# Planned order for SyncE and GpSimd, and the local maxima's transfers moved to GpSimd's queue, in a fused attention and feed-forward kernel

## The chip, the core and the metric

The kernel runs on one core of a Trainium2 chip, with one launch. The metric is the device time in microseconds; lower is better. Engines are named as in the profile: PE (TensorE matmuls), PEld (TensorE weight loads), DVE (VectorE), ACT (ScalarE), POOL (GpSimd), SP (SyncE, which issues nearly all transfers). A "q" behind an engine's name stands for the engine's queue, in which it waits and from which it issues.

## What is computed

A layer norm of `x` (4096 rows of 256) feeds two branches, and both are added to `x`.

The first branch is attention with 16 heads of 16 columns over all 4096 keys, with a softmax over a rational function of the scores:

```python
attn = jnp.einsum('bqhd,bkhd->bhqk', q, k)
sq = attn * attn
w = sq / (nsum - 2.0 * sq + EPS)
w = jax.nn.softmax(w, axis=-1)
out = jnp.einsum('bhqk,bkhd->bqhd', w, v).reshape(B, S, D)
```

The second branch is a two-layer network on the same rows: windowed attention (8 heads of 64, windows of 128 rows that look one window back), then a gated feed-forward with 682 hidden columns, each with a residual.

## The kernel before, in words

**Prologue** (lines 358 to 574, the first 240 us): layer norm, `q`, `k` and `v` of the first branch, stored to DRAM in the layouts that the main part reads.

**Main part.** The first branch is cut into 512 tiles (16 heads, 32 blocks of 128 queries), each in two halves of 2048 keys. For one half: PE makes scores in PSUM (`scores`, L951), ACT squares them into `r` (L955), DVE subtracts 1 (L959), and DVE and ACT together form the weight's exponent in `u` (L963, L972, L978, L981, L985). DVE's `weights` (L993) multiplies and keeps a running maximum in a column of `mm`. When both halves are done, the row maximum of the tile is known, one number for each of 128 queries.

PE turns the exponents round (`turn`, L1014 and L1017): a bf16 matmul first fills the PSUM bank with minus the maximum, and four transposes add the values. For that the maximum is needed as a row, in three bf16 pieces. `maximum` (L998 to L1007) makes it: a transfer of the upper half of the number into row 0 of `mrow`, a subtraction on POOL that leaves the rest, a second transfer, a second subtraction, a third transfer. So a tile has a chain DVE L993, SP, POOL L1007, SP, POOL L1007, SP, PE L1014. ACT then takes the exponential (L1025) and PE multiplies with `v` (`values`, L1036). After four tiles ACT copies the sum to `ob` (L1043) and SP stores it (L1045).

**The second branch** runs through the same engines at the same time, as one long chain of steps (`ffn`, L596 to L915, then `finals`). In its windowed attention, `looked` makes the scores of two heads for 256 rows and DVE (L740) adds a mask and keeps the minimum of the negated scores in `mx`, four columns. POOL splits those minima into three bf16 pieces with four operations (L745 to L748, tiles `fm` and `fmd`), SP moves each piece into a row of `frow` (L751, three transfers), and PE uses `frow` in `summed` (L760) as it uses `mrow` in `turn`. There are 128 such groups: 2 layers, 16 blocks of 256 rows, 4 pairs of heads. The step that uses `frow` is not planned earlier than 10 us after the group (`held[c] = P, mT, plan.now + 10000.0`).

**What sets the order.** A planner written in Python (`Plan`) holds a list of tasks with assumed durations, ranks and buffers, and lets them run on assumed engines when the program is built. It emits each task's instructions at the moment it starts. Tasks for PE, ACT and DVE stand in the program in that order, since the three engines are under `manual_schedule` (L1165). Tasks of the kind "X" take no engine in the plan: `maximum` is one, with 6 us from the weights' end until `turn` may start (`MAX_NS`). SP and POOL are not under the manual schedule before the change. A scheduler of the framework, with a cost model of its own, places their instructions, so their order in the queue is not the order in which the plan emits them.

An engine serves its queue in order. If the first instruction waits, all behind it wait too.

Of the kernel before, what the change touches and what calls it, by code (L numbers as in the profile page):

```python
# [23 lines left out]
NG = S // 512  # L24
# [158 lines left out]
def plan_all(plan, acts, chain, halves):  # L183

    R, PS, U, PE2, PF = Pool(R_BUFS), Pool(3), Pool(U_BUFS), Pool(PE_BUFS), Pool(1)
    acts.pools = dict(r=R, pt=PS, u=U, pe=PE2)
    nothing = lambda: None
    load = [0.0, 0.0]
    subs, last = {}, {"S": None, "P": None, "W": None, "copy": None}

    def rest(i, subs):
        paired = load[0] > load[1]
        load[0] += 10844 if paired else 14448
        load[1] += 12321 if paired else 9050
        acts.mode(i, paired)
        add, D, L, T = plan.add, 2 * i + RANK["D"], 2 * i + RANK["L"], 2 * i + RANK["T"]
        ready = []
        if paired:
            t = add("DVE", 2203, lambda: acts.product(i), D, subs, takes=[(U, i)])
            t = add("DVE", 1135, lambda: acts.positive(i, 0), D, [], [t])  # L200
            t = add("ACT", 1802, lambda: acts.log(i, 0), L, [t])
            t = add("ACT", 1802, lambda: acts.power(i, 0), L, [t])
            ready = [add("DVE", 2203, lambda: acts.signed(i), D, [t])] * 2
        else:
            for h in range(2):
                t = add("DVE", 1135, lambda h=h: acts.positive(i, h), D + h, [subs[h]], [t] if h else [], takes=[] if h else [(U, i)])
                p = add("ACT", 1802, lambda h=h: acts.log(i, h), L + h, [t])
                ready.append(add("ACT", 1802, lambda h=h: acts.power(i, h), L + h, [p]))
        w = None
        for h in range(2):  # L210
            w = add("DVE", 2255, lambda h=h: acts.weights(i, h), T + h, [ready[h]], [w], gives=[(U, i)] if h else [])
        m = add("X", MAX_NS, lambda: acts.maximum(i), 2 * i, [w])
        for n in (2 * i, 2 * i + 1):
            soft(n, m)

    def soft(n, m):
        i, half = divmod(n, 2)
        exps = []
        for z in range(2):
            w = plan.add("PE", 427 + 8 * 109, lambda z=z: acts.turn(n, z), n + RANK["W"] + 0.3 * z, [m], [last["W"]],  # L220
                         takes=[(PS, (n, z, 1))], gives=[(R, n)] if z else [])
            last["W"] = w
            e = plan.add("ACT", 905, lambda z=z: acts.exp(n, z), n + RANK["E"] + 0.3 * z, [w], takes=[(PE2, (n, z))], gives=[(PS, (n, z, 1))])
            exps.append(e)
        fresh = [last["copy"]] if half == 0 and i % 4 == 0 else []
        last["P"] = plan.add("PE", 874, lambda: acts.values(n), n + RANK["P"], exps + fresh, [last["P"]],
                             gives=[(PE2, (n, 0)), (PE2, (n, 1))], mode="C")
        if half and i % 4 == 3:
            last["copy"] = plan.add("ACT", 465, lambda: acts.copied(i), n + RANK["O"], [last["P"]])

    def begin(n):
        sq = []
        for z in range(2):
            s = plan.add("PE", 427, lambda z=z: acts.scores(n, z), n + RANK["S"], [], [last["S"]],
                         takes=[(PS, (n, z, 0))] if z else [(R, n), (PS, (n, z, 0))])
            last["S"] = s
            sq.append(plan.add("ACT", 905, lambda z=z: acts.square(n, z), n + RANK["Q"], [s], gives=[(PS, (n, z, 0))]))
        subs[n] = sub = plan.add("DVE", 1135, nothing, n + RANK["D"], sq, [subs[n - 1]] if n % 2 else [])

        def emit():  # L240
            acts.less(n)
            if n % 2:
                rest(n // 2, [subs.pop(n - 1), subs.pop(n)])
            if n + 8 < halves:
                begin(n + 8)
        sub.emit = emit

    for n in range(min(8, halves)):
        begin(n)

    spent = [0.0]

    def follow(t, step):
        if step is None:
            return
        eng, ns, mode, take, give, at = step
        if eng in ("ACT", "DVE"):
            load[0 if eng == "ACT" else 1] += ns
        due = halves * spent[0] / CHAIN_NS
        spent[0] += ns * PACE[eng]  # L260
        bank = {0: [], 1: [(PF, 0)], 2: [(PS, "f")]}
        u = plan.add(eng, ns, nothing, due + RANK["F"], [t], takes=bank[int(take)], gives=bank[int(give)], mode=mode, at=at)

        def emit():
            follow(u, next(chain, None))
        u.emit = emit

    follow(None, next(chain))
    plan.run()
# [3 lines left out]
def tile_yat_attention_and_local_ffn(ctx: ExitStack, tc: tile.TileContext, io, out):  # L273
# [322 lines left out]
    def ffn():  # L596
        for l in range(DEPTH):
# [63 lines left out]
            for g in range(NGF):  # L661
# [42 lines left out]
                for b in range(2):  # L704
# [4 lines left out]
                                 start=k == 0, stop=k == 1)  # L709
                    yield step("DVE", 600, give=True)  # L710
                    V.tensor_copy(va[:, (2 * g + b) % 3, :, 0:FD], pv.rearrange("p (h d) -> p h d", h=FH))
                if g + 1 < NGF:
                    nxt = fetch(g + 1)
                osum = fa.tile([128, 2, INNER], F32, name="xm2")

                def looked(c):

                    P = fb.tile([128, 2, 2, 256], F32, name="P")
                    mx = fb.tile([128, 4], F32, name="mx")

                    yield step("PE", 1200, "R", take=2)
                    pss = ps_s.tile([128, 2, 2, 256], F32, name=acts.name("pt", "f"))
# [14 lines left out]
                    for e in range(2):  # L737
                        for b in range(2):
                            mk = msk[:, 0 if (g == 0 and b == 0) else 1]
                            V.tensor_tensor_reduce(P[:, e, b], pss[:, e, b], mk, rn[:, 0, b, 2 * c + e:2 * c + e + 1], 3.0e38,  # L740
                                                   ALU.add, ALU.min, mx[:, 2 * e + b:2 * e + b + 1])
                    yield step("X", 0)
                    m3 = fb.tile([128, 3, 4], BF, name="fm3")
                    md = fb.tile([128, 4], F32, name="fmd")
                    G.tensor_copy(m3[:, 0], mx)  # L745
                    G.tensor_tensor(m3[:, 1], mx, m3[:, 0], ALU.subtract)
                    G.tensor_tensor(md, mx, m3[:, 0], ALU.subtract)
                    G.tensor_tensor(m3[:, 2], md, m3[:, 1], ALU.subtract)  # L748
                    mT = frow[c % 2]
                    for c_ in range(3):  # L750
                        nc.sync.dma_start(mT[c_:c_ + 1], m3[:, c_])  # L751
                    held[c] = P, mT, plan.now + 10000.0

                def summed(c):
# [28 lines left out]
                for c in range(5):  # L783
                    if c < 4:
                        yield from looked(c)
                    if c:
                        yield from summed(c - 1)
                oT = fa.tile([128, 4, GT], F32, name="qT")
# [13 lines left out]
                yield step("DVE", 600, give=True)  # L802
                xm = fa.tile([128, 2, D], F32, name="xm")
                V.tensor_tensor(xm, pw, xres, ALU.add)
                nc.sync.dma_start(xm_d[l][g * GT + 1:(g + 1) * GT + 1].rearrange("(t p) c -> p t c", p=128), xm)

            if l == DEPTH - 1:
# [21 lines left out]
            for g in range(NG):  # L829
# [13 lines left out]
                hn = fa.tile([128, 4, D], F32, name="qT")  # L843
                for t in range(4):
                    V.tensor_scalar(hn[:, t], xh[:, t], mv[:, t, 0:1], rstd[:, t:t + 1], ALU.subtract, ALU.mult)
                if g + 1 < NG:
                    nxt = shifted(g + 1)
                h2 = []
                for c in range(2):
                    yield step("PE", 510, take=True)  # L850
# [3 lines left out]
                    yield step("DVE", 725, give=True)  # L854
                    h2.append(fb.tile([128, 512], F32, name="pT"))
                    V.tensor_scalar(h2[c], ph, lngb[:, 0, c:c + 1], lngb[:, 1, c:c + 1], ALU.mult, ALU.add)
                gg = fa.tile([128, 6, 512], F32, name="kv")

                def up(s_, m):
# [36 lines left out]
                if l < DEPTH - 1:  # L896
                    for c in range(2):
# [4 lines left out]
                        yield step("DVE", 600, give=True)  # L902
                        xoT = fb.tile([128, 512], F32, name="pT")
                        V.tensor_copy(xoT, ph)
                        for z in range(2):
                            nc.sync.dma_start(xT_d[l + 1][2 * g + z][c * 128:(c + 1) * 128], xoT[:, z * GT:(z + 1) * GT])
                    for z in range(2):
                        nc.sync.dma_start(xres_d[l + 1][2 * g + z].rearrange("(t p) c -> p t c", p=128), xo[:, 2 * z:2 * z + 2])
                else:
# [2 lines left out]
                    nc.sync.dma_start(xin, acc_d[g].rearrange("(t p) c -> p t c", p=128))  # L912
                    yield step("DVE", 1135)
                    V.tensor_tensor(xo, xo, xin, ALU.add)
                    nc.sync.dma_start(ff_d[g].rearrange("(t p) c -> p t c", p=128), xo)  # L915


# [5 lines left out]
    class Acts:  # L923
# [11 lines left out]
        def scores(self, n, z):  # L935
            i, half = divmod(n, 2)
            h, qt = tiles[i]
            if half == 0 and z == 0:
                if qt == 8 and h + 1 < H:
                    assert self.valued >= 8 * NT * h  # L940
                    load_k(h + 1)
                    load_v(h + 1)
                if qt % 4 == 0 and i // 4 + 1 < len(quads):
                    load_q(*quads[i // 4 + 1])
            if z == 0:
                self.r[n] = hr.tile([128, 2048], F32, name=self.name("r", n))
# [93 lines left out]
        def copied(self, i):  # L1040
            h, qt = tiles[i]
            self.ob = hp.tile([128, 512], F32, name="ob", bufs=1)
            A.copy(self.ob, pav)  # L1043
            if i + 1 < len(tiles):
                nc.sync.dma_start(o_d[qt // 4][h], self.ob)  # L1045
                if h == H - 1:
# [115 lines left out]

    plan = Plan()
    acts = Acts()
    with tc.manual_schedule(engines={mybir.EngineType.PE, mybir.EngineType.Activation, mybir.EngineType.DVE}):  # L1165
        plan_all(plan, acts, chain(), 2 * len(tiles))
        last_rows(acts.ob)

# [56 lines left out]
```

## Time and profile before

| | before |
|---|---|
| time, median of 3 runs | 7330.53 us (7329.86 to 7334.82) |
| time of the profiled execution | 7328.83 us |
| its span, first to last instruction | 7327.0 us |
| granted TensorE clock, mean | 0.981 |
| POOL busy, share of the span | 25% |
| `mrow` transfers on SP (L1004) | 1536, 0.2 KB each |
| `frow` transfers on SP (L751) | 384, 1.0 KB each |

A line of the groups of instructions reads: line, engine, operation, output and inputs, shapes, count, then the busy time in us, the mean of one in ns, and the engine's idle time just before them with what ended it. A line of the waits reads: who waited, for whom, us in total, times, the longest in us. A line of the timeline reads: start in us, duration in us, engine, line, operation, and in brackets the idle time before and what ended it.

### The profile page before, as it was taken

To read this page: it belongs to the slowest core of one execution; us is meant where nothing else is said; L and a number is where in the kernel's file an instruction comes from. 1 tells how busy PE (TensorE), PEld (TensorE's weight loads), DVE (VectorE), ACT (ScalarE), POOL (GpSimd) and SP (SyncE) were. 2 spreads that over 40 slices of the span, in tenths; PEclk is the share of its full clock that TensorE was granted. 3 is DMA by queue.
4 is the path that set the end of the run, shared out by engine and by line. 5 is a ranking of instruction groups with operands and counts; after the bars stand their busy time and mean duration, and the time that the engine had idled before them with its cause. 6 is when DMAs were issued, how large, how long until landed. Compare 5 with 4: busy or idle time off the path is not lost. (4 is left out here: it accounts for less than half of the span.)

```text
span 7327.0 us, 158565 instructions
## 1 busy us (share of the span) xinstructions
PE 6747.6 (92%) x66274; PEld 4786.4 (65%) x67136; DVE 6907.5 (94%) x7307; ACT 6972.8 (95%) x6761; POOL 1806.4 (25%) x1567
## 2 busy tenths in 40 slices
PE   7799999999999998899999999999999999999998
PEld 3466666666676665666666676666666666666665
DVE  8999999999999998899999999999999999899998
ACT  8899999999999998899999999999999999899998
POOL 0123233223332322212223322332232220011210
PEclk9899999999999999999999999999999999999999
DMA  3201010010000111011110010101010023101012
GB/s 130 76 16 21 17 24 15 17 22 17 20 19 15 30 40 26 19 31 24 35 21 19 20 19 17 23 14 25 15 23 15 17 59 87 36 21 31 20 46 77
DMA packets 542303, 223.84 MB, mean 31 GB/s; under 512 B 374988, under 2 KB 514003, under 8 KB 539538
## 3 DMA queue, kind: packets, MB, share of 16 engines
q1 hardware_dynamic: 539650, 212.73, 12.3%
q8 instruction: 527, 8.63, 0.5%
q14 instruction: 190, 1.56, 0.1%
q10 hardware_dynamic: 1936, 0.92, 0.0%
HBM read 124.59 MB, written 88.08 MB: 29 GB/s over the span
## 5 line engine op out<-in xcount | busy, mean ns | idle before, releaser
L1017 PE MATMUL pt<-ident,r 128*128 128x128 f32 x16384 | 2497.5, 276 | 0.0
L1017 PEld LDWEIGHTS pt<-ident,r 128*128 128x128 f32 x16384 | 2082.7, 143 | 577.3 <-issue 199.4
L1025 ACT ACTIVATE pe<-pt 128x1024 f32<-128x1024 f32 x2048 | 2178.8, 1099 | 147.0 <-PE pt L1017 122.5
L955 ACT ACTIVATE r<-pt 128x1024 f32<-128x1024 f32 x2048 | 2120.9, 1104 | 86.5 <-PE pt L951 45.0
L1007 POOL TENSOR_TENSOR mm<-mm 128x1 f32<-128x1 f32 x1024 | 1033.9, 1010 | 4714.3 <-DVE mm L993 4547.7
L1014 PE MATMUL pt<-mrow,neg 128*128 128x512 bf16 x4096 | 1577.6, 385 | 220.8 <-DMA mrow<-mm 108.2
L978 ACT ACTIVATE u<-u 128x2048 f32<-128x2048 f32 x702 | 1395.4, 1997 | 26.8 <-DVE u L972 26.4
L981 ACT ACTIVATE u<-u 128x2048 f32<-128x2048 f32 x702 | 1403.5, 1999 | 0.7
L959 DVE TENSOR_SCALAR r<-r 128x2048 f32<-128x2048 f32 x1024 | 1242.5, 1221 | 65.2 <-ACT r L955 64.8
L993 DVE CUSTOM_DVE_ANT_0 r<-r,u,mm 128x2048 f32<-128x2048 f32 x512 | 1201.3, 2346 | 63.4 <-ACT u L981 58.4
L951 PE MATMUL pt<-K,Q 128*128 128x512 bf16 x3234 | 1013.2, 383 | 199.7 <-ACT pe L1025 129.8
L993 DVE CUSTOM_DVE_ANT_0 r<-r,u 128x2048 f32<-128x2048 f32 x512 | 1169.1, 2283 | 13.0 <-ACT u L981 6.4
L1036 PE MATMUL pv<-pe,vh 128*17 128x128 f32 x32768 | 1074.1, 275 | 21.4 <-ACT ob L1043 7.9
L1036 PEld LDWEIGHTS pv<-pe,vh 128*17 128x17 f32 x32768 | 819.0, 97 | 298.7 <-issue 279.7
L985 DVE SCALAR_TENSOR_TENSOR u<-u 128x2048 f32<-128x2048 f32 x322 | 736.1, 2286 | 74.6 <-ACT u L981 73.8
L951 PEld LDWEIGHTS <-Q 128*128 128x128 bf16 x4096 | 375.4, 99 | 574.6 <-issue 393.6
L963 DVE TENSOR_TENSOR u<-r,r 128x2048 f32<-128x2048 f32 x322 | 735.6, 2285 | 1.9
L1014 PEld LDWEIGHTS <-neg 128*128 128x128 bf16 x4096 | 406.7, 99 | 350.7 <-issue 249.6
L972 DVE TENSOR_SCALAR u<-r 128x2048 int32<-128x2048 int32 x380 | 457.1, 1219 | 1.6 <-DMA q_d<-pb 1.5
L972 DVE TENSOR_SCALAR u<-u 128x2048 int32<-128x2048 int32 x322 | 394.4, 1225 | 7.5
L863 PE MATMUL pf<-pT,wqkv_s 128*128 128x512 f32 (+1 forms) x768 | 367.5, 601 | 4.2 <-DVE kv L883 1.5
L745 POOL CAST fm<-mx 128x4 bf16<-128x4 f32 x128 | 216.9, 1695 | 481.2 <-DVE mx L740 470.5
(211 smaller groups left out, 6005.1 us busy)
## 6 DMA issues: line engine op xcount, KB each, us to landing
o<-ob SPq DMA_DIRECT2D x127, 256.0 KB
mrow<-mm SPq DMA_DIRECT2D x1536, 0.2 KB
Q<-q_d SPq DMA_DIRECT2D x256, 48.0 KB
K<-k_d SPq DMA_DIRECT2D x32, 384.0 KB
tab<-in_tables_dram SPq DMA_DIRECT2D x32, 256.0 KB
xres<-xres SPq DMA_DIRECT2D x32, 256.0 KB
xm<-xm SPq DMA_DIRECT2D x32, 256.0 KB
P<-xm SPq DMA_DIRECT2D x32, 256.0 KB
```

The lines of the kernel that those rows point to most:

```text
L951: T.matmul(ps[:, j * 512:(j + 1) * 512], lhsT=Q[:, (qt % 4) * 128:(qt % 4 + 1) * 128], rhs=K[:, o + j * 512:o + (j + 1) * 512], start=True ...
L955: A.activation(self.r[n][:, z * 1024:z * 1024 + 1024], self.pt.pop((n, z)), AF.Square)
L959: V.tensor_scalar(self.r[n], self.r[n], 1.0, 1.0e-9, ALU.subtract, ALU.subtract)
L972: V.tensor_scalar(self.part(i, h).bitcast(I32), src.bitcast(I32), 0x7FFFFFFF, None, ALU.bitwise_and)
L978: A.activation(self.part(i, h), self.part(i, h), AF.Ln)
L981: A.activation(self.part(i, h), self.part(i, h), AF.Exp, scale=-2.0)
L993: V.tensor_tensor_reduce(self.r[2 * i + h], self.r[2 * i + h], self.part(i, h), 1.0 if self.paired[i] else -0.5, init, ALU.mult, ALU.max, ...
L1007: G.tensor_tensor(mm[:, c_ + 1:c_ + 2], mm[:, c_:c_ + 1], head[:, 2 * c_ + 1:2 * c_ + 2], ALU.subtract)
L1014: T.matmul(pt[:, 512 * b:512 * b + 512].rearrange("p (s n) -> p s n", s=4), lhsT=neg1, rhs=self.mT[i].unsqueeze(1).broadcast_to([128, 4, 1 ...
L1017: T.matmul(pt[:, 512 * b + j * 128:512 * b + (j + 1) * 128], lhsT=self.r[n][:, o + j * 128:o + (j + 1) * 128], rhs=ident, is_transpose=Tru ...
L1025: A.activation(pe, self.pt.pop((n, z)), AF.Exp)
L1036: T.matmul(pav[32 * (j % 4):32 * (j % 4) + 17, (qt % 4) * 128:(qt % 4) * 128 + 128], lhsT=vh[h % 2][:, kt, :], rhs=pe[:, j * 128:(j + 1) * ...
```

## The change

SP and POOL come under the manual schedule too, so that their instructions stand in the order in which the plan emits them. What was emitted together with its producer is emitted when the plan thinks that the source is there: the store of `ob` becomes an X task behind the copy (`stored`), the stores of `xm`, `xoT` and `xo` get an X step of no length before them, and three loads are emitted later: `fetch(g + 1)` after the second `looked`, `shifted(g + 1)` after the transposes, the next `Q` one tile later.

The minima are split with three POOL operations in place of four: two subtractions of the upper halves (which are read in place as bf16) and one copy of all twelve columns. The three transfers to `frow` are issued by POOL and not by SP.

```diff
+            plan.add("X", 0, lambda: acts.stored(i), n, [last["copy"]])
...
-                if g + 1 < NGF:
-                    nxt = fetch(g + 1)
                 osum = fa.tile([128, 2, INNER], F32, name="xm2")
...
-                    mx = fb.tile([128, 4], F32, name="mx")
+                    mx = fb.tile([128, 3, 4], F32, name="mx")
...
                     yield step("X", 0)
                     m3 = fb.tile([128, 3, 4], BF, name="fm3")
-                    md = fb.tile([128, 4], F32, name="fmd")
-                    G.tensor_copy(m3[:, 0], mx)
-                    G.tensor_tensor(m3[:, 1], mx, m3[:, 0], ALU.subtract)
-                    G.tensor_tensor(md, mx, m3[:, 0], ALU.subtract)
-                    G.tensor_tensor(m3[:, 2], md, m3[:, 1], ALU.subtract)
+                    hd = mx.bitcast(BF).rearrange("p j (n w) -> p j n w", w=2)[:, :, :, 1]
+                    for c_ in range(2):
+                        G.tensor_tensor(mx[:, c_ + 1], mx[:, c_], hd[:, c_], ALU.subtract)
+                    G.tensor_copy(m3, hd)
                     mT = frow[c % 2]
                     for c_ in range(3):
-                        nc.sync.dma_start(mT[c_:c_ + 1], m3[:, c_])
+                        nc.gpsimd.dma_start(mT[c_:c_ + 1], m3[:, c_])
...
                     if c < 4:
                         yield from looked(c)
+                    if c == 1 and g + 1 < NGF:
+                        nxt = fetch(g + 1)
...
                 V.tensor_tensor(xm, pw, xres, ALU.add)
+                yield step("X", 0)
                 nc.sync.dma_start(xm_d[l][g * GT + 1:(g + 1) * GT + 1].rearrange("(t p) c -> p t c", p=128), xm)
...
-                if g + 1 < NG:
-                    nxt = shifted(g + 1)
                 h2 = []
...
+                if g + 1 < NG:
+                    nxt = shifted(g + 1)
                 gg = fa.tile([128, 6, 512], F32, name="kv")
...
-                if qt % 4 == 0 and i // 4 + 1 < len(quads):
+                if qt % 4 == 1 and i // 4 + 1 < len(quads):
                     load_q(*quads[i // 4 + 1])
...
             A.copy(self.ob, pav)
+
+        def stored(self, i):
+            h, qt = tiles[i]
             if i + 1 < len(tiles):
                 nc.sync.dma_start(o_d[qt // 4][h], self.ob)
...
-    with tc.manual_schedule(engines={mybir.EngineType.PE, mybir.EngineType.Activation, mybir.EngineType.DVE}):
+    with tc.manual_schedule(engines={mybir.EngineType.PE, mybir.EngineType.Activation, mybir.EngineType.DVE, mybir.EngineType.SP, mybir.EngineType.Pool}):
```

Two more X steps stand before the stores of `xoT` (L906) and of `xo` (L915).

More of the change, by code (lines that the diff above doesn't have):

```diff
@@ L740, in looked @@
                             V.tensor_tensor_reduce(P[:, e, b], pss[:, e, b], mk, rn[:, 0, b, 2 * c + e:2 * c + e + 1], 3.0e38,
-                                                   ALU.add, ALU.min, mx[:, 2 * e + b:2 * e + b + 1])
+                                                   ALU.add, ALU.min, mx[:, 0, 2 * e + b:2 * e + b + 1])
                     yield step("X", 0)
                     m3 = fb.tile([128, 3, 4], BF, name="fm3")
-                    md = fb.tile([128, 4], F32, name="fmd")
[L745 to L748, printed above, removed]
+                    hd = mx.bitcast(BF).rearrange("p j (n w) -> p j n w", w=2)[:, :, :, 1]
+                    for c_ in range(2):
+                        G.tensor_tensor(mx[:, c_ + 1], mx[:, c_], hd[:, c_], ALU.subtract)
+                    G.tensor_copy(m3, hd)
                     mT = frow[c % 2]
                     for c_ in range(3):
-                        nc.sync.dma_start(mT[c_:c_ + 1], m3[:, c_])
+                        nc.gpsimd.dma_start(mT[c_:c_ + 1], m3[:, c_])
                     held[c] = P, mT, plan.now + 10000.0
@@ L904, in ffn @@
                         V.tensor_copy(xoT, ph)
+                        yield step("X", 0)
                         for z in range(2):
@@ L914, in ffn @@
                     V.tensor_tensor(xo, xo, xin, ALU.add)
+                    yield step("X", 0)
                     nc.sync.dma_start(ff_d[g].rearrange("(t p) c -> p t c", p=128), xo)
```

## The prediction

> **What bounds the kernel now.** I read the page's first part first, then the waits, then the timeline around single waits.
>
> ```profile
> span 7327.0 us, 158565 instructions
> ...
> PE 6747.6 (92%) x66274; PEld 4786.4 (65%) x67136; DVE 6907.5 (94%) x7307; ACT 6972.8 (95%) x6761; POOL 1806.4 (25%) x1567
> ```
>
> Three engines are nearly full, and ACT is idle for only 7327.0 - 6972.8 = 354 us. By the windows, 55 us of that lie in the first 250 us and 40 us in the last 327 us, which leaves some 260 us in the middle for any change of order to win. The change touches waits for transfers alone, so the question is how much of this idle time hangs on a transfer:
>
> ```profile
> PE pt L951 <- ACT pe L1025: 129.8, 151, 3.6
> ...
> PE pt L1014 <- DMA mrow<-mm: 108.2, 38, 8.8
> PE pt L1014 <- ACT pe L1025: 72.5, 124, 4.1
> ```
>
> `turn` waits 108.2 us for `mrow`, in 38 places. No other transfer of the main part has a wait of weight: PE waits 4.2 us for `pT`, and nobody for `frow`, `Q`, `K` or `vh`. These 108.2 us are real time: around the 38 stalls the trace has ACT idle for 116 us and DVE for 103 us. So I count a microsecond of this stall as a microsecond.
>
> Why is `mrow` late? I lined up, for all 512 tiles, the end of L993, the two POOL subtractions, the three issues on SP and the start of `turn`. With free queues the third issue ends 2.8 us after the weights (median), and `turn` can start 2.45 us behind that. The 38 stalls fall into three kinds. (a) POOL is still busy with the minima when the weights end: 12 stalls, 37.5 us. (b) POOL starts at once, but its two subtractions take long: 17 stalls, 54.6 us. (c) SP is busy elsewhere: 9 stalls, 16.2 us. A stall of kind (a), on POOL and then on PE:
>
> ```profile
> 1563.29 2.25 POOL L745 CAST fm<-mx 128x4 bf16<-128x4 f32 x1 [10.38 <-DVE mx L740]
> 1565.61 1.08 POOL L746 TENSOR_TENSOR fm<-mx,fm 128x4 bf16<-128x4 f32 x1
> 1566.64 2.25 POOL L747 TENSOR_TENSOR fmd<-mx,fm 128x4 f32<-128x4 f32 x1
> 1568.97 2.13 POOL L748 TENSOR_TENSOR fm<-fmd,fm 128x4 bf16<-128x4 f32 x1
> 1571.06 1.31 POOL L1007 TENSOR_TENSOR mm<-mm 128x1 f32<-128x1 f32 x2
> ```
>
> ```profile
> 1572.30 0.60 PE L1017 MATMUL pt<-ident,r 128*128 128x128 f32 x4
> 1577.69 0.61 PE L1014 MATMUL pt<-mrow,neg 128*128 128x512 bf16 x1 [4.80 <-DMA mrow<-mm]
> ```
>
> The weights ended at 1565.49, behind the minima at 1563.2. The four operations held POOL until 1571.1, and PE stood for 4.80 us. The same line shows that each POOL operation, which does 128x4 numbers, ends where a DVE instruction ends (at 1565.5, 1566.6, 1568.8, 1571.0): they last 0.19 us when DVE leaves room and 1.1 or 2.2 us when it does not.
>
> **The change, part by part.**
>
> *Order of PE, ACT and DVE.* The two built programs have the same instructions on them; set side by side without their waits they give 59 lines of difference among 7262 on DVE and 82 among 6737 on ACT. I cost this at nothing. The X steps have no length in the plan.
>
> *Order of SP.* SP no longer stands on a full `Q` or `hT` buffer (L338 227.6 us and L631 94.5 us in SP's waits, all for PE), since the loads are emitted after the last reader. It also loses 384 transfers, for which it waited 433.7 + 278.8 + 118.1 us on POOL. This is kind (c), 16.2 us. In the new order SP can still stand before an ACT copy that comes later than planned, so I leave 5 us of it. Moved loads have cover: `Q` is issued three tiles (some 40 us) ahead, `hT` and `tab` two pairs of heads ahead, `xh` a whole block ahead. `K` and `vh` are needed some 20 tiles later. If that cover went, each miss would be a few us.
>
> *Order of POOL.* The minima and the subtractions are both released by DVE, whose order is the plan's, so POOL no longer stands before a minimum that is not there (470.5 us of POOL's waits are L745 for `mx`). But it is now strict first come, first served: a tile whose weights end just behind a minimum waits for the whole group.
>
> *Length of the group.* This decides.
>
> ```profile
> L1007 POOL TENSOR_TENSOR mm<-mm 128x1 f32<-128x1 f32 x1024 | 1033.9, 1010 | 4714.3 <-DVE mm L993 4547.7 <-DVE rn L703 34.4 <-DMA Q<-q_d 23.1
> L745 POOL CAST fm<-mx 128x4 bf16<-128x4 f32 x128 | 216.9, 1695 | 481.2 <-DVE mx L740 470.5 <-DMA mrow<-mm 10.6
> L746 POOL TENSOR_TENSOR fm<-mx,fm 128x4 bf16<-128x4 f32 x128 | 203.2, 1587 | 10.3
> L747 POOL TENSOR_TENSOR fmd<-mx,fm 128x4 f32<-128x4 f32 x128 | 200.9, 1570 | 0.0
> L748 POOL TENSOR_TENSOR fm<-fmd,fm 128x4 bf16<-128x4 f32 x128 | 152.2, 1189 | 10.0
> ```
>
> Before: 1695 + 1587 + 1570 + 1189 = 6.0 us, 6.2 with the gaps. After: three operations, which by the start of today's fourth end 5.0 us after the minimum, plus three transfers that POOL issues itself, at d each. The trace has no transfer issued by POOL. From below, d is SP's price for the same transfer:
>
> ```profile
> L751 SPq DMA_DIRECT2D frow<-fm x384: 468/469/1003, 353.8 to 5951.2; - x192
> ```
>
> From above it is the longest POOL operation of the group, 2.34 us (L748). I take 1.06 us, the median of L1007 and of L748, the nearest rows: one instruction of that queue beside the same DVE work. The group is then 5.0 + 3 x 1.06 = 8.2 us.
>
> With the times of the trace I let POOL serve weights and groups in the order of DVE's ends, subtractions at their own measured lengths, `mrow` ready 0.53 + 2.45 us behind the second, and summed by how much it comes after PE's demand, moving all that follows. 52 of the 512 tiles end their weights within 6.2 us of a minimum, 62 within 8 us, 73 within 9.5 us. The stall that comes out:
>
> | group, us | 5.0 | 6.4 | 7.4 | 8.0 | 8.2 | 8.6 | 9.5 | 11.9 |
> |---|---|---|---|---|---|---|---|---|
> | d, us | 0 | 0.47 | 0.8 | 1.0 | 1.06 | 1.2 | 1.5 | 2.3 |
> | stall, us | 57 | 74 | 98 | 128 | 138 | 163 | 229 | 459 |
>
> The first column is nearly kind (b) alone, which the change leaves.
>
> *`frow` itself.* `summed` (L760) starts 9.95 us after the minimum at the earliest, 10.5 us at the tenth percentile, 15.1 at the median. The third transfer is now issued at 8.2 us, and 2 us on it is there: no stall at d = 1.06, some tens of us from d = 1.5 (in the table).
>
> *The sum.* 7328.8 us (span 7327.0 and 1.8 around it) + (138 - 108) + 5 = 7364, say **7365 us**. The profiled execution lies 1.7 us under the median, which I neglect. By the bounds: 7328.8 + 74 - 108 = 7295 at d = 0.47, and 7328.8 + 459 - 108 = 7680 at d = 2.3.
>
> *A rule against the change.* The trace shows POOL operations held until a DVE instruction ends, and L959 and L972 alone (1242.5 + 457.1 + 394.4 us) are 28.6% of the span. [...]
>
> **Rivals.**
>
> *POOL issues cheaply, faster.* At d up to 0.75 the group is at most 7.2 us and the stall 57 to 93 us: 7278 to 7314 us. For: SP needs 0.47 us, and without DVE a POOL operation takes 0.19 us. Against: the medians above.
>
> *It cancels out.* d from 0.75 to 0.95, or queues that nobody waits for: 7314 to 7343.
>
> *POOL's queue, slower (the forecast).* From d = 0.95 on the group is longer than what the better order wins back: 7344 at d = 0.95, 7450 at d = 1.5.
>
> *DVE starves POOL.* From d = 2 on, `frow` comes late as well in half the groups and two queues stall: over 7580 us. For: the operations of 5 to 11 us in kind (b). Against: those are subtractions at 2.8 to 3.6 ms, outside the windowed attention.
>
> **How the numbers follow.** Forecast 0.48, cheap 0.29, cancelling 0.15, starving 0.08. A measurement tells 0.2%, or 14.7 us, from no change, so faster 0.29, same 0.15, slower 0.56. The range 7285 to 7460 takes in d from 0.3 to 1.5 and leaves out the starving case and the last of the cheap one; of slower alone it would be 7345 to 7460.
>
> **What would show it.** The new rows of POOL for `frow` give d: under 0.75 the forecast is wrong, and over 0.95 it is right in sign. PE's wait for `mrow` should read 130 to 160 us. SP's waits for POOL's `fm` and for PE at L338 should be gone. A new wait of PE L760 for `frow` would be the starving case. If d is near 1 and the wait for `mrow` still falls, the queue sum is wrong; if the wait falls and the time does not, the one-to-one step is.

## The result and the profile after

| | before | after |
|---|---|---|
| time, median | 7332.67 us (7329.86 to 7339.64, 4 runs) | 7414.24 us (7413.16 to 7415.05, 4 runs) |
| time of the profiled execution | 7328.83 us | 7413.93 us |

The ratio is 1.011, 95% interval 1.0092 to 1.0127: slower by 81.6 us. The forecast was 7365, so the sign was right and the size under half. Lines have moved: `turn` is now L1017 and L1020, the `mrow` transfers L1007, POOL's subtractions L1010, the minima L745 and L746, their transfers L749, the use of `frow` L758.

The head of the page of after. PE, PEld, DVE and ACT do the same work as before, within 0.5% of their busy time, in 85 us more; POOL, which now issues the 384 transfers, is busy 5% longer:

```profile
span 7412.0 us, 158291 instructions
...
PE 6779.5 (91%) x66272; PEld 4801.6 (65%) x67136; DVE 6909.7 (93%) x7307; ACT 6977.5 (94%) x6761; POOL 1895.1 (26%) x1823
```

What the forecast turned on, the price d of a transfer that POOL issues, is in the view of the tile `frow` (after "x384": shortest, median and longest, in ns):

```profile
L749 POOL DMA_DIRECT2D frow<-fm x384: 537/546/1547, 358.5 to 5980.1; - x192
...
  DMA frow<-fm: 1.2, 2
```

The mean is 704 ns, so d is 0.70 us, on the cheap side, and PE waited for `frow` only 1.2 us in two places. The waits of after look as forecast all the same (130 to 160 us for `mrow`):

```profile
ACT pe L1028 <- PE pt L1020: 169.3, 136, 9.4
PE pt L1017 <- DMA mrow<-mm: 147.8, 55, 11.2
```

That is 39.6 us more than before, half of the loss, and it does not lie where POOL's groups lie. I lined up the 512 tiles of both traces by the start of `turn`. The table has the delay against before, in us, and the `mrow` stalls in the stretch (the last delay is that of the last `turn`; over the whole span it is 85.0 us):

| stretch (tiles) | delay at its end | added in it | `mrow` stalls before, after |
|---|---|---|---|
| windowed attention of layer 1 (0 to 159) | 7.2 | 7 | 31.6, 20.5 |
| its feed-forward (160 to 239) | 18.0 | 11 | 29.7, 38.4 |
| start of layer 2 (240 to 255) | 26.3 | 8 | 8.2, 7.0 |
| windowed attention of layer 2 (256 to 415) | 28.0 | 2 | 24.1, 23.9 |
| first `finals` (416 to 431) | 61.9 | 34 | 1.1, 28.7 |
| feed-forward of layer 2 (432 to 495) | 69.4 | 7 | 5.3, 9.3 |
| second `finals` (496 to the end) | 85.5 | 16 | 8.4, 20.0 |

The windowed attention, where POOL has its groups, lost 9 us in 320 tiles. Of these the 7 us of the first row are in part the spread of single executions: the runs e2, e5 to e8 and e14 to e16 below, which have SP in the same written order up to there, lie 0.5 to 6.0 us behind at tile 160. The first `finals`, where POOL has none, lost 34 in 16. The windows of that stretch, before and then after (busy us of PE, PEld, DVE, ACT and POOL, then the granted clock, the DMA share and GB/s):

```profile
5979.00:6200.00 221.00, 204.21 (x1956) 133.62 (x1982) 205.46 (x202) 208.80 (x185) 18.56 (x30) 0.98 0.36 98
```

```profile
6007.00:6262.00 255.00, 215.88 (x1956) 140.70 (x1982) 206.04 (x202) 209.76 (x185) 18.55 (x30) 0.91 0.39 95
```

The same instructions, 34 us more. SP's timeline in it, after:

```profile
6020.38 0.49 SPq L1103 DMA_DIRECT2D rec<-msk  x1
6023.87 0.29 SPq L1105 DMA_DIRECT2D pT<-rec  x1
6024.21 1.80 SPq L1007 DMA_DIRECT2D mrow<-mm  x3
...
6049.09 0.29 SPq L1105 DMA_DIRECT2D pT<-rec  x1
6049.43 0.64 SPq L1088 DMA_DIRECT2D fsq<-o  x1
6050.13 0.62 SPq L1089 DMA_DIRECT2D P<-o  x1
...
6053.84 0.57 SPq L1089 DMA_DIRECT2D P<-o  x1
6054.45 0.47 SPq L1093 DMA_DIRECT2D qT<-in_L_attn_inputs_q_dram  x1
6055.03 1.81 SPq L1007 DMA_DIRECT2D mrow<-mm  x3
```

Two things stand in front of `mrow`. At 6020.4 SP stores `rec`, the reciprocal of the softmax's sum, and then stands 3 us before the load that reads it back from DRAM into `pT`; the tile whose weights ended at 6019.24 gets its `mrow` issued at 6024.2. At 6049.4 SP issues the nine loads of the next block, 1.6 MB, in 5.5 us; the weights of another tile end at 6052.44, its `mrow` is issued from 6055.0 to 6056.8, and then its 0.2 KB transfers stand once more, in the DMA queue (q1) that carries the loads too: the 512 packets of 1 KB of the last load start between 6056.4 and 6064.4 us, the 384 packets of 2 bytes of `mrow` between 6058.2 and 6064.6:

```profile
6066.92 0.59 PE L1017 MATMUL pt<-mrow,neg 128*128 128x512 bf16 x1 [6.78 <-DMA mrow<-mm]
6067.30 1.06 PE L1020 MATMUL pt<-ident,r 128*128 128x128 f32 x4
...
6069.86 0.60 PE L1020 MATMUL pt<-ident,r 128*128 128x128 f32 x4
```

10 us lie between the issue and PE's start, against 2.7 us in the median of the tiles of this trace that PE waited for. In the kernel before, the scheduler had put `mrow` between these transfers:

```profile
6015.12 1.31 SPq L1082 DMA_DIRECT2D hT<-o  x2
6016.53 0.51 SPq L1097 DMA_DIRECT2D rec<-msk  x1
6017.12 0.66 SPq L1087 DMA_DIRECT2D qT<-in_L_attn_inputs_q_dram  x1
6017.87 0.59 SPq L1083 DMA_DIRECT2D wqkv_s<-o  x1
6018.56 0.43 SPq L1099 DMA_DIRECT2D pT<-rec  x1
6019.04 0.59 SPq L1083 DMA_DIRECT2D wqkv_s<-o  x1
6019.68 0.57 SPq L1082 DMA_DIRECT2D hT<-o  x1
6020.94 2.76 SPq L1004 DMA_DIRECT2D mrow<-mm  x3
6023.79 1.91 SPq L338 DMA_DIRECT2D Q<-q_d  x3
6027.47 0.61 SPq L1083 DMA_DIRECT2D wqkv_s<-o  x1
```

### The profile page after: what moved, and what is told of

It is laid out like the page before. It is cut to its first block, busy times and chain, and to the rows that moved or that the text cites. A ratio compares the mean times of both kernels' runs of the same rounds, so it can differ in the third digit from the quotient of the medians.

```text
span 7412.0 us, 158291 instructions
## 1 busy us (share of the span) xinstructions
PE 6779.5 (91%) x66272; PEld 4801.6 (65%) x67136; DVE 6909.7 (93%) x7307; ACT 6977.5 (94%) x6761; POOL 1895.1 (26%) x1823
## 5 line engine op out<-in xcount | busy, mean ns | idle before, releaser
L1020 PE MATMUL pt<-ident,r 128*128 128x128 f32 x16384 | 2510.0, 277 | 0.0
L1020 PEld LDWEIGHTS pt<-ident,r 128*128 128x128 f32 x16384 | 2093.2, 143 | 573.4 <-issue 197.1
L1010 POOL TENSOR_TENSOR mm<-mm 128x1 f32<-128x1 f32 x1024 | 1010.4, 987 | 4738.7 <-DVE mm L996 4497.5
L1017 PE MATMUL pt<-mrow,neg 128*128 128x512 bf16 x4096 | 1585.2, 387 | 262.3 <-DMA mrow<-mm 147.8
L962 DVE TENSOR_SCALAR r<-r 128x2048 f32<-128x2048 f32 x1024 | 1243.3, 1221 | 67.6 <-ACT r L958 67.2
L954 PE MATMUL pt<-K,Q 128*128 128x512 bf16 x3232 | 1013.1, 383 | 203.5 <-ACT pe L1028 130.2
L1017 PEld LDWEIGHTS <-neg 128*128 128x128 bf16 x4096 | 408.1, 100 | 404.5 <-issue 278.2
L745 POOL TENSOR_TENSOR mx<-mx 128x4 f32<-128x4 f32 x256 | 416.2, 1626 | 450.6 <-DVE mx L739 440.2
```

Of the source, the lines that this page charges most:

```text
L954: T.matmul(ps[:, j * 512:(j + 1) * 512], lhsT=Q[:, (qt % 4) * 128:(qt % 4 + 1) * 128], rhs=K[:, o + j * 512:o + (j + 1) * 512], start=True ...
L962: V.tensor_scalar(self.r[n], self.r[n], 1.0, 1.0e-9, ALU.subtract, ALU.subtract)
L1010: G.tensor_tensor(mm[:, c_ + 1:c_ + 2], mm[:, c_:c_ + 1], head[:, 2 * c_ + 1:2 * c_ + 2], ALU.subtract)
L1017: T.matmul(pt[:, 512 * b:512 * b + 512].rearrange("p (s n) -> p s n", s=4), lhsT=neg1, rhs=self.mT[i].unsqueeze(1).broadcast_to([128, 4, 1 ...
L1020: T.matmul(pt[:, 512 * b + j * 128:512 * b + (j + 1) * 128], lhsT=self.r[n][:, o + j * 128:o + (j + 1) * 128], rhs=ident, is_transpose=Tru ...
```

## The experiments

Theory A: the loss is SP's written order, above all in `finals`. Rival B: the forecast, POOL's queue. All runs together (the ratio is to the kernel before, measured beside each run, with its 95% interval):

| run | time, us | ratio | PE waits for `mrow`, us |
|---|---|---|---|
| before, after | 7333, 7414 | 1, 1.011 | 108.2, 147.8 |
| e1 SP free | 7336.3 | 1.0002 (0.9992 to 1.0011) | 111.4 |
| e2 POOL free | 7413.3 | 1.0112 (1.0095 to 1.0129) | 157.9 |
| e3 both free | 7336.5 | 1.0002 (0.9992 to 1.0011) | 113.6 |
| e4 rows by SP | 7481.6 | 1.0198 (1.0182 to 1.0213) | 203.5 |
| e5 no trip | 7383.0 | 1.0067 (1.0052 to 1.0082) | 120.6 |
| e6 burst after rows | 7392.8 | 1.0079 (1.0064 to 1.0094) | 109.3 |
| e7 both mends | 7441.6 | 1.0148 (1.0131 to 1.0165) | 108.1 |
| e8 loads by ACT | 7472.4 | 1.0190 (1.0175 to 1.0205) | 103.8 |
| e9 minima always behind | 7367.3 | 1.0046 (1.0029 to 1.0063) | 58.1 |
| e10 SP free, rows by SP | 7333.0 | 0.9996 (0.9987 to 1.0006) | 111.1 |
| e11 store after rows | 7409.8 | 1.0104 (1.0089 to 1.0119) | 150.6 |
| e12 store and trip | 7387.5 | 1.0073 (1.0058 to 1.0088) | 117.1 |
| e13 minima if due | 7267.3 | 0.9908 (0.9893 to 0.9923) | 43.8 |
| e14 fetch early | 7419.9 | 1.0115 (1.0100 to 1.0130) | 151.8 |
| e15 trip and fetch | 7383.5 | 1.0065 (1.0049 to 1.0082) | 123.4 |
| e16 with room | 7396.5 | 1.0082 (1.0067 to 1.0097) | 121.1 |
| e17 minima if due, SP in order | 7336.3 | 1.0001 (0.9992 to 1.0011) | 99.9 |
| e18 minima if due, rows by SP | 7264.3 | 0.9904 (0.9887 to 0.9920) | 52.4 |

### Whose order it is: e1 to e4, e10

```diff
-    with tc.manual_schedule(engines={... DVE, mybir.EngineType.SP, mybir.EngineType.Pool}):
+    with tc.manual_schedule(engines={... DVE, mybir.EngineType.Pool}):      # e1
+    with tc.manual_schedule(engines={... DVE, mybir.EngineType.SP}):        # e2
+    with tc.manual_schedule(engines={... DVE}):                             # e3
...
-                        nc.gpsimd.dma_start(mT[c_:c_ + 1], m3[:, c_])
+                        nc.sync.dma_start(mT[c_:c_ + 1], m3[:, c_])         # e4; e10 with e1's line
```

> The changed kernel, except that SyncE is not in the written order: the framework's scheduler places its transfers again, as in the kernel before; PE, ACT, DVE and GpSimd keep the written order and GpSimd still transfers frow. Theory A (the loss is SP's strict order: a load or a store that is issued where the plan stands holds up the mrow transfers behind it, most of all in the two finals stages, +34 and +16 us of the +85 us of span): 7325 to 7350 us, and PE's wait for mrow back to some 105 to 125 us from 147.8. Rival B (the forecast: GpSimd's queue is longer by three transfers of 0.70 us a group and first come, first served): 7395 to 7415 us, PE's wait for mrow still about 140 us.

> The changed kernel, except that GpSimd is not in the written order; SP is, and GpSimd still transfers frow. The other engines' instructions stand as in the changed kernel. Theory A: nothing to gain here, 7400 to 7420 us. Rival B: the part of GpSimd's written order is regained, 7330 to 7385 us, with fewer mrow stalls that wait for GpSimd.

> The changed kernel with neither SP nor GpSimd in the written order: what is left of the change is the subtraction in place with one copy for the three rows, the frow transfers on GpSimd, and the transfers' places in the program. Theory A: like the run with SP alone free, 7320 to 7350 us. Rival B, with the transfers of 0.70 us as the cost: 7370 us or more. A third theory C (the moved places themselves cost, whoever orders SP): also near 7400 us here.

> The changed kernel with the 384 frow transfers on SyncE's queue again, in the written order; GpSimd only makes the rows. Theory A: SP's queue, already in order, gets 384 more transfers of some 0.5 us, each standing for GpSimd's copy: slower than the changed kernel, 7420 to 7460 us. Rival B: GpSimd's groups are shorter by 2.1 us, 7370 to 7400 us.

> The kernel with SP free (7336 us), with the frow transfers on SP again: against the run with SP free it tells what GpSimd's transfers are worth without SP's strict order. Theory D: the group on GpSimd is shorter by 2.1 us, so the stalls that wait for GpSimd in a minima group fall from 45 us towards the 26 of the kernel before, and those that wait for SP rise from 5 to about 16 us; sum 7320 to 7330 us. Rival E (the transfers on GpSimd spare as much on SP as they cost): 7333 to 7340 us. If SP's queue was the bound here as in written order (+67 us there): 7350 us or more.

Theory A is shown and B falls. In e1 PE, DVE, ACT and POOL have the same instructions in the same order as in after; only SP's order differs, and 78 us are gone. Lined up as above, e1 never lies more than 8.2 us behind the kernel before, and the first `finals` adds nothing:

```profile
5982.00:6202.00 220.00, 202.79 (x1957) 133.02 (x1983) 205.67 (x202) 209.04 (x184) 18.51 (x30) 0.98 0.36 98
```

POOL's order alone is worth nothing either way (e2, e3). The transfers on POOL spare 67 us, but only where SP is in written order (e4 against after: 384 more transfers behind POOL's copies, and the wait for `mrow` at 203.5 us in place of 147.8); with SP free they cost 3 us, within the spread (e10 against e1). So theory C, that the moved places cost by themselves, falls with e3.

### Which transfers in SP's order: e5 to e8

```diff
# e5: in middle, the two transfers go behind the additions, each at a time of its own
-            return g, w, fin, last, de, on, plan.now + 8000.0
+            yield step("X", 0, at=plan.now + 2500.0)
+            nc.sync.dma_start(rec_d[c][g][0:w // 16].rearrange("h (a n) -> h a n", a=8), dn[0:w // 2])
+            yield step("X", 0, at=plan.now + 3000.0)
+            de = fb.tile([8, 512], F32, name="pT")
+            nc.sync.dma_start(de[0:w // 16], rec_d[c][g][0:w // 16])
+            return g, w, fin, last, de, on, plan.now + 3000.0
...
# e6: front's nine loads become loads(); maximum() runs what waits, behind its third transfer
+            acts.after_rows(loads)
...
# e8: front's nine loads
-                nc.sync.dma_start(
+                nc.scalar.dma_start(
```

> The changed kernel; in the finals the store of rec and the load that reads it back are each put into SP's order when the planner expects their source to be ready (2.5 us after the reduction starts, then 3 us later), so that SP stands neither for DVE (34.5 us in 16 waits before) nor for the round trip through DRAM (27.7 us in 16). Theory A1 (SP's standing holds the mrow rows): the mrow stalls of the two finals fall, 7375 to 7395 us. Theory A2 (the nine loads of a block are what holds them, in SP's queue and on the DMA queue): little, 7400 to 7415 us.

> The changed kernel; in the finals the nine loads of a block (1.6 MB) are put into SP's order just behind the next three mrow transfers, so that the next mrow is some 13 us away when they start. Theory A2: most of the 34 + 16 us of the finals is regained, 7365 to 7385 us. Theory A1: the round trip is still there, 7395 to 7410 us.

> The two edits together (loads behind the mrow rows; no standing for DVE and the round trip). Theories A1 and A2 both: the finals cost what they cost in the kernel before, 7360 to 7375 us; what is left over the kernel before is the start of layer 2 and the feed-forward stages.

> The changed kernel; the nine loads of a block are issued by ACT instead of SP, at the same places in the plan, so SP's queue is free of them and the 1.6 MB arrive at the same time over another queue. Theory A2a (they hold mrow by SP's issue time, 5.5 us a block, and by the order in one DMA queue): the mrow stalls of the finals go, against 8 times 9 issues on ACT in each finals, some 40 us in all of which part shows: 7370 to 7410 us, PE's wait for mrow near 110 us. Theory A2b (they hold mrow by filling the DMA engines, whatever the queue): the stalls stay, PE's wait for mrow above 140 us, and the time is 7420 us or more.

e5 regains 31 us and e6 21: both the round trip and the burst hold `mrow` (in the first `finals` its stalls fall from 28.7 to 9.8 and to 1.6). The steps that these two put in also move some 150 to 215 instructions of ACT and of DVE to other places in their order, from the first `finals` on, so the time that each regains is not SP's alone. e8 leaves that order as it is. It shows that the burst does its harm through SP's queue or the DMA queue behind it, which it does not tell apart, and not by filling the DMA engines: the same 1.6 MB over ACT's queue leave 1.7 us of `mrow` stalls there. ACT pays for it, since its work now stands behind these transfers in its own queue:

```profile
ACT pe L1028 <- DMA P<-o: 30.9, 5, 7.9
```

e7 is a plain miss. The `mrow` stalls of the first `finals` are gone, and a wait of 4.2 us in the kernel before is now a large one:

```profile
PE pf L1135 <- DMA pT<-rec: 41.8, 10, 9.3
```

The loads came later by up to a tile, the reductions, `rec` and its load later with them, and PE, in its own written order, stood for `pT`. Here a stall that a later transfer took from one place turned up at the place that needs it.

### The rest of SP's order: e11, e12, e14 to e16

```diff
# e11: stored()'s transfer, and what it tells finals, goes behind the next mrow transfers
+                self.after_rows(put)
...
# e14: for layer 2, hT and tab ahead of the planned wait
+            if l:
+                nxt = fetch(0)
             yield step("X", 12000 if l else 45000)
```

e12 is e11 with e5, e15 is e14 with e5, e16 is e15 with e6 for the first `finals` and margins of 12 and 6 us in place of 8 and 3.

> The changed kernel, in written order everywhere; the store of ob is put into SP's order behind the next three mrow transfers, so that SP does not stand for ACT's copy (510.8 us in 94 waits). Theory A3 (a store that stands for its source holds the loads behind it, as at the start of layer 2, +8 us, and in the feed-forward stages, +17): 7390 to 7402 us, and the waits for the tables at 3690 us gone. Rival: SP stands at mrow instead, with nothing gained: 7410 to 7416 us.

> The changed kernel with the store behind the mrow rows and, in the finals, rec's store and load placed at the times their source is expected (alone 7383 us). If the two losses are apart from each other they add: 7360 to 7372 us; if the store had no part, 7380 to 7386 us.

> The changed kernel; at the start of layer 2 the first loads of hT and tab are put into SP's order with the layer's weights, ahead of the planned wait of 12 us, not behind it where the plan puts their first use. Theory A4 (in strict order a load is issued where the plan stands, so one that stands next to its first use is exposed in full: 8.4 and 11.3 us of waits at 3697 us): both waits gone, 7402 to 7408 us. Rival A3 (SP's standing for ob was the cause): no change, 7412 to 7416 us.

> The changed kernel with the early first loads of layer 2 and, in the finals, rec's store and load placed when their source is expected (alone 7383 us). If both losses are separate: 7370 to 7380 us.

> The kernel of the run before this one, and in the first finals the nine loads of a block behind the next mrow, with 12 us instead of 8 until their first use and 6 us instead of 3 before and behind rec's load. The runs with 8 and 3 us lost the mrow stalls and got new waits of PE for rec and of DVE for the loads instead. Theory G (strict order costs what the written margins fail to cover): mrow stalls and new waits both small in the first finals, 7355 to 7370 us. Rival: more room only lengthens the chain of the finals, 7380 us or more.

Theory A3 falls as a main term (e11 gains 4 us, e12 nothing over e5); the store has a part in the feed-forward of layer 1, where e11 and e12 add 4 us and the other runs of this order 8 to 11. A4 as I had put it falls too: in e14 the waits at the start of layer 2 are still there, and e15 adds nothing to e5 (7383.5 against 7383.0, where 7370 to 7380 was expected). SP's timeline of e14 says why:

```profile
3675.55 1.05 SPq L913 DMA_DIRECT2D xres<-qT  x2
3676.64 0.91 SPq L601 DMA_DIRECT2D wqkv_s<-in_L_ffn_wqkv_dram  x1
...
3681.79 2.35 SPq L611 DMA_DIRECT2D b_s<-in_L_ffn_b_dram  x1
...
3685.72 4.21 SPq L619 DMA_DIRECT2D scl<-in_L_ffn_q_scale_dram  x2
3689.97 0.91 SPq L619 DMA_DIRECT2D scl<-in_L_ffn_k_scale_dram  x2
3690.92 0.43 SPq L623 DMA_DIRECT2D hT<-xT  x1
```

Once the last stores of layer 1 are out, SP issues the layer's weights for 14 us without a pause; `hT` stands behind them wherever the plan put it by less than that. In e1 the scheduler has most of these weights out before 3625 us: of them only `fwo_s` and `xm` are issued between 3625 and 3690 us. That it is this backlog which costs the 8 us is argued, not shown: no run took it away by itself. What costs the rest in the two feed-forward stretches stays open as well.

e16 halves the first `finals`' stalls (13.3 us) and takes that stretch from 34 us to nothing, but the feed-forward behind it then starts 71 us later than in after and loses 33 us. So theory G falls as a price: room in one stage is paid in the next, since the chain of the second branch is one chain.

### The place of the minima group: e9, e13, e17, e18

e1 left a question: its wait for `mrow`, 111.4 us, is 3 us above that of the kernel before. I sort the `mrow` stalls of all runs by one rule: kind (a), POOL's first subtraction starts over 1.5 us behind the weights; else kind (c), SP's last issue ends over 1 us behind the second subtraction; else kind (b). In us:

| kind | before | after | e1 | e4 | e5 | e6 | e8 | e13 | e17 |
|---|---|---|---|---|---|---|---|---|---|
| (a) POOL late | 37.5 | 40.9 | 45.5 | 29.3 | 43.0 | 39.4 | 40.3 | 0 | 1.6 |
| (b) subtractions slow | 58.6 | 58.4 | 60.9 | 71.4 | 51.5 | 58.0 | 58.5 | 38.3 | 38.8 |
| (c) SP late | 12.1 | 48.5 | 5.0 | 102.8 | 26.1 | 11.9 | 5.0 | 5.5 | 59.5 |

The change's added wait is kind (c), 36.4 of 39.6 us, and it goes with SP's order (e1). The forecast's longer queue, kind (a), is there with 3 us in after and 8 in e1. (Some expectations speak of 26 and 16 us of (a) and (c) in the kernel before; the rule gives 37.5 and 12.1.)

The planner knows when a tile's weights have begun, and so can keep the group out of the way:

```diff
# e13, on e1: the group (two subtractions, copy, three transfers) becomes minima()
+                    acts.after_rows(minima)
...
         def weights(self, i, h):
             if h == 0:
+                self.soon += 1        # maximum() takes it back and runs what waits
...
+        def after_rows(self, f):
+            if not self.soon:         # e9 always waits for the next maximum()
+                f()
+            else:
+                self.later.append(f)
```

> The kernel with SP free (7336 us) and one thing more: the minima group on GpSimd (two subtractions, the copy, three transfers, some 7 us) is put into its order just behind the next tile's own subtractions, not where the plan stands. In the run with SP free, 25 of the 47 mrow stalls (45 us) began while GpSimd was in a minima group. Theory D (a group in first-come order is worth these 45 us): fewer than 8 such stalls, PE's wait for mrow 70 to 80 us instead of 111, 7295 to 7315 us. Rival: the rows of minima come later, by up to 14 us, and the wait moves to PE's use of frow or lengthens the chain: 7330 us or more.

> The kernel with SP free (7336 us); the minima group is put behind the next tile's subtractions only if that tile's weights have already begun in the plan (its maximum is then at most some 5 us away), and else at once. The run that always put it behind had 58 us of mrow stalls in place of 111 and was still 31 us slower, its last frow some 170 us later. Theory D (the group's place costs the kind (a) stalls, 45 us; its lateness cost the chain of the local layers): half of these stalls go, the chain keeps its time, 7310 to 7325 us. Rival F (a mrow stall that waits for GpSimd is not worth its length, since the chain's other work fills or absorbs it): 7330 to 7342 us although the stalls fall.

> The changed kernel with SP and GpSimd both in written order, and the minima group placed as in the run of 7267 us (behind the next tile's subtractions if that tile's weights have begun). That run had lost 67.6 us of PE's wait for mrow (111.4 to 43.8) and 69 us of time. If the place of the group and SP's order are two separate terms: 7414 - 69 + 0 = 7345 us, within 10. If the freed GpSimd stalls turn into waits for SP, which is late at the same moments: 7365 us or more.

> The kernel of 7267 us (SP free, the minima group placed by the plan) with the frow transfers on SP again: what the transfers on GpSimd are worth when the group no longer stands in the way. If nothing, as in the pair without the placing (7336 and 7333 us): 7260 to 7275 us. If the shorter group gains more: 7250 to 7260 us; if SP's 384 further transfers now hold the mrow rows, which are earlier: 7275 to 7300 us.

e13 beats both kernels, by more than I expected: 7267.3 us. Its wait for `mrow`, with kind (a) down from 25 stalls to none and (b) from 61 to 38 us:

```profile
PE pt L1037 <- DMA mrow<-mm: 43.8, 21, 5.4
```

67.6 us of wait went (from e1's 111.4), and 69 us of time. The rival F, that these stalls are not worth their length, falls. But only the 45.5 us of kind (a) are what the rule is about. The rule also makes the plan place other steps elsewhere: of the 7307 instructions of DVE some 1300 stand in another order than in e1. The 22.6 us less of kind (b) were not foreseen; that they come with that other order is likely and not shown, for no run holds the order and moves the group alone. In e9 the wait fell by 53.3 us and the time rose by 31; the group came up to a tile later, PE waited for `frow`, and the last group was served at 6130 us in place of 5953, so that the feed-forward of layer 2 began at 6383 us in place of 6199:

```profile
PE pf L765 <- DMA frow<-fm: 27.4, 23, 5.2
```

e17 speaks for two separate terms: with SP in written order the same placing gains 78 us and lands on the kernel before (7345 expected). Its profiled execution was the slowest of its ten, so its 99.9 us of wait stand beside 7354.7 us. e18 shows that the transfers on POOL have no part in e13's gain.

## Why the prediction was right and wrong

*A microsecond of `mrow` wait is a microsecond: held, with a limit.* e1 and e13 differ by 67.6 us of wait and 69 us of time; e1 and the kernel before by 3 and 1. The limit is what else moves: in e9, e7 and e8 the wait fell and the time rose, because the chain of the second branch came later or another engine stood. And the change itself cost twice its added wait. Part of the other half has names: DVE waited 11.3 us for `tab`, PE 8.4 for `xres` and 6.5 for `Q`, which neither had waited for before, and PE was busy 11.7 us longer in the first `finals` for the same matmuls. That these make up the whole is not shown.

*Order of PE, ACT and DVE, nothing: held* (e3).

*Order of SP: this step failed.* It was priced as kind (c), 16.2 us, of which "I leave 5 us", so as a gain of 11, since "moved loads have cover". The moved loads did have cover, but for one wait of 6.5 us for `Q`. Kind (c) was the right term and grew fourfold: 12.1 us in the kernel before, 48.5 in after, 5.0 in e1. I priced the transfers that the diff moves. But to put an engine under a written order moves all its transfers, those too whose lines are unchanged: the nine loads, the store and the load of each block of `finals`, the weights of layer 2. The scheduler had hoisted and interleaved these, and the diff shows none of them. Measured: a loss of 78 us (after against e1) in place of a gain of 11. Mending the round trip alone regains 31 us and the burst alone 21; the two do not add (e7), so these are not shares of the 78.

*Order of POOL and length of the group: the sizes were off, and they cancelled.* With d = 0.70 the group is 2 x 1.63 + 1.50 + 3 x 0.70 = 6.9 us, and 7.3 with the gaps between its parts, not 8.2. My table gives about 96 us of stall for 7.3 and so 7317 us; e1 has 111.4 us and 7336. So the forecast's cost of a transfer was too high and the queue sum beneath it too low. The kernel before could have told: for its group of 6.2 us the table gives some 72 us, and its trace had 92 of kinds (a) and (b) by the prediction's own count. I took a measured 108 from a modelled 138, so that this shortfall went into the forecast as a gain. What the sum leaves out I have not found. The gain that I named, that POOL no longer stands before a minimum, did not come either: 440.2 us of such waits against 470.5.

*`frow` has no stall: right*, 1.2 us.

*The rivals.* "POOL issues cheaply" had the right d and the wrong time (7278 to 7314), for the same failed step. None of the rivals put the loss on SP. Their times, and the bounds, leave out the 5 us for SP that the forecast itself has in its sum. That POOL's operations of over 5 us lie at 2.8 to 3.6 ms was read too narrowly: the trace has two such stalls at 6.8 ms too, also outside the windowed attention.

*The check was too weak.* "PE's wait for `mrow` should read 130 to 160 us" came true at 147.8 by luck, from another cause: 36 us of it go with SP's order alone. A total that fits proves little; the place of the stalls (16 tiles without any POOL group) told it at once.

*The rule against the change.* POOL's transfers took 537 to 1547 ns beside a DVE that is 93% busy, 704 in the mean, and landed 2.1 us after their start in the median, 4.7 at most. The longest of the 384 is under d = 2, from which the starving case was reckoned, and PE's wait for `frow` stayed at 1.2 us: no starving here.

## What to carry to other kernels

When an engine goes from a scheduler to a written order, price every instruction of its queue, not the lines of the diff: list its bursts and its store-then-load pairs, and ask which urgent transfer stands behind each. A written order is worth having where it uses what the planner knows: here the kernel with the one rule "not while a tile's maximum is due" was 69 us faster, with SP left to the scheduler. A deferral must be as short as the reason for it, or the wait returns at the consumer, as in e7 (41.8 us for `pT`) and e9 (27.4 us for `frow`). And a model is held against the kernel before first; a forecast then takes model from model.

## What the runs showed of the hardware

An `mrow` of three transfers of 0.2 KB, issued behind 1.6 MB into the same DMA queue, was used 10 us after its issue (2.7 us in the median of the tiles that PE waited for), and of 28.7 us of stalls in that stretch 1.7 were left when that bulk went over ACT's queue (e8): here the order in SP's queue, or in the DMA queue behind it, decided, not the load on the DMA engines.

The stand of 6.78 us cost PE more than its length. In the lines of PE's timeline above, behind it four transposes take 1.06 us, and 0.60 us again some 3 us later; the granted clock is 0.50 from 6066.9 to 6069.8 us and 1.00 from 6069.9 to 6072.9. Over the first `finals` the same 1956 matmuls were busy for 215.9 us in place of 204.2, at a granted clock of 0.91 in place of 0.98.
